# Half of a cross-attention's probabilities transposed by VectorE and five DMAs through DRAM, in place of TensorE

## The chip, the cores and the metric

The kernel runs on one core of one Trainium2 chip, in one launch. The metric is the device time of that launch in microseconds (us). All arithmetic is in 32-bit floats.

A core has five engines, each with its own in-order stream of instructions: TensorE (PE in the profile; its weight loads are a second row, PEld), VectorE (DVE), ScalarE (ACT), GpSimd (POOL) and SyncE (SP, which here only issues DMAs). They wait for each other through semaphores. SBUF is the on-chip memory of 128 partitions, PSUM the accumulators that TensorE writes, in banks of 512 floats a partition.

## The reference

Sixteen sequences, each with 128 queries of width 512 and a context of 2048 rows of width 512. Three layers follow each other:

```
x = x + xattn(layernorm(x), ctx)      # 16 heads of 32; k, v from ctx
x = x + mamba_and_mlp(layernorm(x))   # selective scan of 16 states, then an MLP of 2048
x = x + moe(layernorm(x))             # one shared and one gated expert product
# inside xattn, per sequence and head:
attn = softmax(q @ k.T * scale)       # 128 x 2048
out  = attn @ v                       # 128 x 32
```

What the change touches is `attn @ v`. It sums over the 2048 context rows, so the exponentials, which come out of the softmax with queries on partitions, must be turned until context rows lie on partitions.

## The kernel before

**Steps.** One loop, `for u in range(last)`, writes the whole order of work by hand; no scheduler moves an instruction afterwards. The first 256 steps (NU) are the attention: step u takes sequence u // 16, context block u // 4 % 4 of 512 rows, and head group u % 4 of four heads (`split`). Beside it, step u carries pieces of everything else: the k and v projections of the next context block (a seven-product scheme in place of eight, line 240), the Mamba layer of earlier pairs of sequences (input projection, scan), and after step 256 the MLP and the experts. From step 54 on (32 + LAG), each step also holds a piece of a scan. Dictionaries (`late`, `inner`, `middle`, `loads` and others) say in which step each piece goes; many pieces return every 32 steps, and below r is u % 32.

**One step on TensorE**, in order: the scores of four heads, one bank each (line 302); the weighting of the step before (`weighted(u - 1)`, line 346); two products of a projection (`x_products`, line 240, into `pa` and `pc`); sixteen transposes of 128x128, four to a bank (`turn`, line 333, a matrix product with the identity); the step's `late` pieces (line 531: Mamba's input projection; line 472: the output projection; line 716: Mamba's output; line 459: factors turned; line 399: queries); then `y_products`, one product in odd steps and two in even ones (line 240 again).

**One step on the others.** VectorE: the maxima of the four heads (line 310), the first half of the scan (687, its product with C at 690, a small memset at 666), the sum that empties `pc` (`x_sums`: line 260 for k, 270 for v), one of the four turned chunks copied out of PSUM (336), the second half of the scan, then sums of the projection and odds and ends. ScalarE: four exponentials (320), a copy that empties `pa` (280), the decays of the scan (673), three turned chunks (338), and every fourth step a copy of the weighted sums `avp` (360). GpSimd: differences of context tiles (232), the scan's inputs (652) and the sums of its outputs (703).

**SP's queue** is in order too. A step's loads stand at the top of the step, among them `load_bc` (601, two rows of 512 KB), context tiles (154), and weights into six shared buffers `ws` (504, 509, 167, 169). A load into a buffer still in use makes SP wait for the engine that uses it, and everything behind it in SP's queue waits too.

**Banks.** Four banks `s0` to `s3` hold a step's scores, then its turned chunks; `late` pieces borrow them in between, and the accumulator bank `avp` is borrowed in one step of four.

Of the kernel before, what the change touches and what calls it, by code (L numbers as in the profile page):

```python
# [8 lines left out]
FP = mybir.dt.float32  # L9
# [6 lines left out]
P = 128  # L16
B, NQ, D, S = 16, 128, 512, 2048
H, HD = 16, 32
KC = D // P
# [6 lines left out]
GT = GB * NQ  # L26
# [2 lines left out]
MT = MB * NQ  # L29
NE = 7  # L30
NH = 4


@with_exitstack
def perceiver_layer(ctx: ExitStack, tc: tile.TileContext, a: dict, out: bass.AP):
    nc = tc.nc

    const = ctx.enter_context(tc.tile_pool(name="const", bufs=1))
    dram = ctx.enter_context(tc.tile_pool(name="dram", bufs=1, space=DRAM))

    ident = const.tile([P, P], FP, tag="ident", name="ident")
# [14 lines left out]
    zd = [dram.tile([NQ, D], FP, tag=f"zd{b}", name=f"zd{b}") for b in range(B)]  # L56
    xnd = [dram.tile([NQ, D], FP, tag=f"xnd{b}", name=f"xnd{b}") for b in range(B)]
    bcd = [dram.tile([2 * DS, GT], FP, tag=f"bcd{g}", name=f"bcd{g}") for g in range(B // GB)]

    mv = const.tile([P, B, 2], FP, tag="mv", name="mv")  # L60
    rstd = const.tile([P, B], FP, tag="rstd", name="rstd")
# [43 lines left out]
    NU = B * SB * 4  # L105
# [3 lines left out]
    with ExitStack() as es:  # L109
        acon = es.enter_context(tc.tile_pool(name="acon", bufs=1))  # L110
        keep = es.enter_context(tc.tile_pool(name="keep", bufs=2))
        ssm = es.enter_context(tc.tile_pool(name="ssm", bufs=2))
        psum = es.enter_context(tc.tile_pool(name="psum", bufs=1, space=PSUM))
        att = es.enter_context(ExitStack())
        pool = att.enter_context(tc.tile_pool(name="att", bufs=2))
# [19 lines left out]
        scale = float(HD) ** -0.5  # L135
        nc.vector.tensor_scalar_mul(bq, bq, scale)

        ctx_t, kts, vts, qts, prs, pts, avs, stats, xts = ({} for _ in range(9))
# [43 lines left out]
        def split(u):  # L182
            return u // 16, u // 4 % 4, u % 4
# [92 lines left out]
                product(of, g, i, ps)  # L276

        def hold(key, g, pa, tag):
            t = pool.tile([P, 2, 256], FP, tag=tag, name=f"{tag}{key}{g}", bufs=1)
            nc.scalar.copy(t, pa)  # L280
            held[key] = t

# [43 lines left out]
                )  # L326
            prs[u] = pr

        def turn(u, i, bank):

            ps = heads(banks[bank])
            for j in range(4):
                nc.tensor.transpose(ps[:, j, :], prs[u][:, j, i * P : (i + 1) * P], ident)  # L333
            pT = pool.tile([P, 4, P], FP, tag="pT", name="pT", bufs=4)
            if i == 2 and u % 16 > 2:
                nc.vector.tensor_copy(pT, ps)  # L336
            else:
                nc.scalar.copy(pT, ps)  # L338
            pts[u, i] = pT

        def weighted(u):

            b, sb, hg = split(u)
            for i in range(4):
                for j in range(4):
                    nc.tensor.matmul(  # L346
                        avp[j * HD : (j + 1) * HD, hg, :],
                        vts[u // 4, hg // 2, i // 2][
                            :, i % 2, hg % 2 * P + j * HD : hg % 2 * P + (j + 1) * HD
                        ],  # L350
                        pts[u, i][:, j, :],
                        start=(i == 0),
                        stop=(i == 3),
                    )
            for i in range(4):
                del pts[u, i]
            del prs[u]
            if hg == 3:
                t = keep.tile([P, 4, P], FP, tag="avs", name=f"avs{b}_{sb}", bufs=4)
                nc.scalar.copy(t, avp)  # L360
                avs[b, sb] = t


        def moments_of(b):
# [21 lines left out]
        def turned(b, ps):  # L386
            xn = xts.pop((b, "n"))
            for kc in range(KC):
                nc.tensor.transpose(heads(ps)[:, kc, :], xn[:, kc * P : (kc + 1) * P], ident)
            xnT = keep.tile([P, KC, P], FP, tag="fx", name="xnT", bufs=3)  # L390
            nc.vector.tensor_copy(xnT, heads(ps))
            xts[b, "t"] = xnT

# [55 lines left out]
        fxs = {}  # L449

        def spread_out(b, sb):
            fx = keep.tile([P, H, HD], FP, tag="fx", name="fx", bufs=3)
# [110 lines left out]
        def silu_first(g, ec, ts):  # L563

            v = ts[g, ec]
            t = ssm.tile([P, GT], FP, tag="sg", name="sg", bufs=4)
# [591 lines left out]
        early = {}  # L1158
        late, after, inner, middle, loads, head, behind, between = ({} for _ in range(8))

        def put(where, u, f):
            where.setdefault(u, []).append(f)

        for b in range(B):
            s = 16 * b
            if b:
                put(loads, s - 8, lambda b=b: load_x(b))
                put(loads, s - 5, lambda b=b: load_w(0, b))
                put(inner, s - 8, lambda b=b: moments_of(b))
                put(middle, s - 7, lambda b=b: root_of(b))  # L1170
                put(inner, s - 7, lambda b=b: normal(b))
                put(late, s - 4, lambda ps, b=b: queries(b, ps))
            e = s + 16
            put(loads, e + 5, lambda b=b: load_w(3, b))
            put(inner, e - 1, lambda b=b: joined(b))
            put(inner, e, lambda b=b: joined_first(b))
            put(middle, e + 1, lambda b=b: shares(b))
            put(inner, e + 1, lambda b=b: joined_second(b))
            put(head, e + 2, lambda b=b: joined_third(b))
            for sb in range(SB):  # L1180
                put(inner, e + 2 + (sb > 0), lambda b=b, sb=sb: spread_out(b, sb))
                put(late, e + 3 + (sb > 0), lambda ps, b=b, sb=sb: scaled(b, sb, ps))
            put(late, e + 6, lambda ps, b=b: attended(b, ps))
            put(middle, e + 7, lambda b=b: root_of(b))
            put(inner, e + 7, lambda b=b: normed(b))
            put(late, e + 8, lambda ps, b=b: z_turned(b, ps))
# [38 lines left out]
        put(inner, NU, lambda: give_back(flat(pa)))  # L1225


        ways = (("k", pa, pc, "u2"), ("v", halves(banks[0]), halves(banks[1]), "u2v"))

        def first_products(of, ph):  # L1230
            x_products(of, 0, ph, *dict((w[0], w[1:3]) for w in ways)[of])
# [33 lines left out]
            y_sums(of, 0, 0, sa, sc, tag)  # L1265
        load_w(3, -1)

        bvx = keep.tile([P, KC, P], FP, tag="fx", name="bvx", bufs=3)
# [16 lines left out]
        for u in range(last):  # L1285
# [33 lines left out]
            for f in early.get(u, ()):  # L1319
                f()  # L1320
            if u == NU + 8:
                load_wex()
            for f in head.get(u, ()):
# [27 lines left out]


            after_turns = late.get(u, ())
            places = [banks[(3 + i) % 4] for i in range(len(after_turns))]
            if live and after_turns:
# [9 lines left out]
            taken = sum(any(p is b for b in banks) for p in places)  # L1365
# [105 lines left out]
```

## Time and profile before

| | |
|---|---|
| runs | 3762.42, 3763.41, 3765.85 us (median 3763.41) |
| profiled execution, first to last instruction | 3760.5 us; no time of its own around that is recorded, and the median is 2.9 us above it |
| scores of step 0, scores of step 255 (start) | 41.1 us, 3075.3 us |
| mean step, u from 96 to 127 | 12.19 us |
| busy time of VectorE in such a step | 9.75 us |
| granted TensorE clock | 0.998 of full speed |
| DMA | 548.42 MB, 146 GB/s over the span |

The profile has rows by group (line, engine, operation, output and inputs; count; busy time and mean ns of one; idle time before and what ended it), a timeline in order of time, windows (busy time of each engine in a stretch) and rows by DMA issue (count, KB, median us from issue to landing). A mean of one instruction includes its overlap with the next: four maxima of 683 ns each take 2.48 us together. Where two groups share an engine, the timeline's start times give the true pace.

### The profile page before, as it was taken

How to read it: one execution, taken by the hardware profiler on the slowest of the kernel's cores; microseconds unless marked ns; L12 is line 12 of the kernel's file. 1: busy time of each engine (PE TensorE's matmuls, PEld its weight loads, DVE VectorE, ACT ScalarE, POOL GpSimd, SP SyncE). 2: the span in 40 equal slices, each digit the busy share in tenths (PEclk: the TensorE clock that was granted, in tenths of full speed). 3: DMA queues.
4: the chain of work that ended last, by engine and by line, in shares of the span. 5: the costliest groups of instructions: out<-in, count | busy, mean ns of one | idle time of the engine just before them, and what ended most of it. 6: DMA issues, size and time to landing. Idle time of an engine off the chain costs nothing.

```text
span 3760.5 us, 70389 instructions
## 1 busy us (share of the span) xinstructions
PE 3722.9 (99%) x26120; PEld 2851.7 (76%) x26120; DVE 2706.2 (72%) x4854; ACT 2446.9 (65%) x5848; POOL 2112.4 (56%) x1969
## 2 busy tenths in 40 slices
PE   9999999999999999999999999999999999999999
PEld 7878787778777887888787878787778776655655
DVE  3444445887878777877788778877887877778843
ACT  4555556777767776777677767776777775545431
POOL 2111213676767666765666666766675667567820
PEclk9999999999999999999999999999999999999999
DMA  3111122344444535353534453445444448676752
GB/s 102 35 40 43 49 71 83 127 152 150 132 165 142 158 115 186 124 165 116 190 124 149 136 184 128 150 135 172 141 151 139 162 166 312 205 267 244 248 191 82
DMA packets 343225, 548.42 MB, mean 146 GB/s; under 512 B 24368, under 2 KB 227408, under 8 KB 342624
## 3 DMA queue, kind: packets, MB, share of 16 engines
q1 hardware_dynamic: 342432, 543.27, 43.5%
q8 instruction: 206, 3.38, 0.4%
q14 instruction: 139, 1.14, 0.1%
q0 software_dynamic: 448, 0.63, 0.1%
HBM read 527.29 MB, written 16.52 MB: 145 GB/s over the span
## 4 chain that ended last, share of the span: by engine, by line
PE 94%; DVE 2%; DMA 1%; ACT 1%; issue 1%; POOL 0%; SPq 0%; DVEq 0%; ACTq 0%; POOLq 0%
PE pa L240 24%; PE pc L240 17%; PE bank L333 12%; PE bank L302 7%; PE avp L346 7%; PE bank L531 5%; PE bank L942 4%; PE bank L911 2%; PE bank L1043 2%; PE bank L472 2%; PE avp L399 1%; PE bank L716 1%; PE pc L716 1%; PE avp L942 1%; PE pa L911 1%; PE pc L531 1%
## 5 line engine op out<-in xcount | busy, mean ns | idle before, releaser
L310 DVE TENSOR_REDUCE nm<-bank 128x1 f32<-128x512 f32 x1024 | 635.5, 683 | 225.2 <-PE bank L302 225.0
L703 POOL TENSOR_TENSOR ysum<-ysum,w 128x512 f32<-128x512 f32 x384 | 500.2, 1303 | 487.4 <-DVE hst L666 309.0
L320 ACT ACTIVATE pr<-bank,nm 128x512 f32<-128x512 f32 x1024 | 690.6, 688 | 90.9 <-DVE nm L310 85.3
L652 POOL TENSOR_TENSOR w<-dx,bc 128x512 f32<-128x512 f32 x512 | 655.9, 1302 | 8.9
L687 DVE TENSOR_TENSOR_SCAN hst<-hst,w 128x512 f32<-128x512 f32 x459 | 561.1, 1222 | 42.8 <-ACT hst L673 33.6
L338 ACT COPY pT<-bank 128x512 f32<-128x512 f32 x816 | 434.4, 586 | 177.2 <-PE bank L333 173.2
L673 ACT ACTIVATE hst<-dt,alog 128x254 f32<-128x254 f32 x918 | 439.4, 479 | 112.0 <-DVE hst L666 95.8
L333 PE MATMUL bank<-ident,pr 128*128 128x128 f32 x4096 | 508.2, 273 | 3.3 <-ACT pr L320 2.8
L333 PEld LDWEIGHTS bank<-ident,pr 128*128 128x128 f32 x4096 | 468.2, 141 | 47.1 <-issue 11.1
L346 PEld LDWEIGHTS avp<-pT,v 128*32 128x32 f32 x8192 | 208.0, 109 | 194.4 <-issue 176.6
L690 DVE TENSOR_TENSOR w<-hst,bc 128x512 f32<-128x512 f32 x459 | 317.4, 692 | 20.8 <-DMA bc<-bcd 5.2
L232 POOL TENSOR_TENSOR t<-c,c 128x512 f32<-128x512 f32 x128 | 163.1, 1274 | 257.6 <-PE pc L240 253.5
L302 PE MATMUL bank<-kt,qT 32*128 32x512 f32 x2048 | 296.0, 641 | 0.5 <-ACT pT L338 0.5
L346 PE MATMUL avp<-pT,v 128*32 128x128 f32 x8192 | 276.7, 276 | 0.0
L240 PE MATMUL pa<-t,ks 128*128 128x256 f32 x1024 | 248.6, 386 | 0.0
L240 PE MATMUL pa<-vs,t 128*128 128x256 f32 x1008 | 244.7, 386 | 0.0
L240 PEld LDWEIGHTS pa<-vs,t 128*128 128x128 f32 x1008 | 185.4, 190 | 34.6 <-issue 10.1
L240 PEld LDWEIGHTS pa<-t,ks 128*128 128x128 f32 x1024 | 184.8, 190 | 35.2 <-issue 11.6
L320 ACT ACTIVATION_READ_ACCUMULATOR pr<-bank,nm 128x1 f32 x1024 | 210.2, 205 | 0.0
L336 DVE COPY pT<-bank 128x512 f32<-128x512 f32 x208 | 143.9, 692 | 87.3 <-PE bank L333 85.6
L531 PE MATMUL bank<-zT,win 128*128 128x256 f32 x808 | 185.1, 379 | 0.0
L232 POOL TENSOR_TENSOR t<-c,t 128x512 f32<-128x512 f32 x128 | 163.7, 1279 | 36.1 <-issue 19.2
(320 smaller groups left out, 6889.0 us busy)
## 6 DMA issues: line engine op xcount, KB each, us to landing
bc<-bcd SPq DMA_DIRECT2D x512, 512.0 KB, 4.3
c<-in_ctxT_dram SPq DMA_DIRECT2D x256, 256.0 KB, 4.4
wf<-in_w_dram SPq DMA_DIRECT2D x124, 512.0 KB, 6.8
wqo<-in_wqkvo_dram SPq DMA_DIRECT2D x128, 256.0 KB, 4.8
win<-in_win_dram SPq DMA_DIRECT2D x128, 256.0 KB, 4.3
wout<-in_wout_dram SPq DMA_DIRECT2D x128, 256.0 KB, 4.2
x<-in_x_dram SPq DMA_DIRECT2D x16, 256.0 KB, 4.0
x1d<-x SPq DMA_DIRECT2D x16, 256.0 KB, 2.1
```

The lines of the kernel that those rows point to most:

```text
L240: nc.tensor.matmul(ps[:, r, :], l[:, kc, r * P : (r + 1) * P], m[:, kc, :], start=(i in (1, 2, 5) and r == 0 and kc == 0), stop=(r == 1 an ...
L302: nc.tensor.matmul(banks[j], qts[b][rows, hg, :], kts[u // 4, hg][rows, :], start=True, stop=True)
L310: nc.vector.tensor_reduce(stats[b][0][j][:, sb, hg : hg + 1], banks[j], AX.X, ALU.max, negate=True)
L320: nc.scalar.activation(pr[:, j, :], banks[j], AF.Exp, bias=nm[j][:, sb, hg : hg + 1], accum_out=sm[:, sb, h : h + 1],)
L333: nc.tensor.transpose(ps[:, j, :], prs[u][:, j, i * P : (i + 1) * P], ident)
L338: nc.scalar.copy(pT, ps)
L346: nc.tensor.matmul(avp[j * HD : (j + 1) * HD, hg, :], vts[u // 4, hg // 2, i // 2][:, i % 2, hg % 2 * P + j * HD : hg % 2 * P + (j + 1) * HD],
L531: nc.tensor.matmul(ps, w[:, kc, :], zTs[g][:, kc, :], start=(kc == 0), stop=(kc == KC - 1))
L652: nc.gpsimd.tensor_tensor(w, dx.unsqueeze(1).to_broadcast([P, NH // 2, GT]), bcs[g * 32 + r, 0][:, i * NH // 2 : (i + 1) * NH // 2, :], AL ...
L673: nc.scalar.activation(bt(h[:, k, :])[:, :, 1:], bt(dt)[:, :, 1:], AF.Exp, scale=aneg[:, ec, n : n + 1],)
L687: nc.vector.tensor_tensor_scan(flat, flat, w.rearrange("p n t -> p (n t)"), 0.0, ALU.mult, ALU.add)
L703: nc.gpsimd.tensor_tensor(s, s, w, ALU.add)
```

## The change

Of each step's four heads, heads 0 and 1 (NP = 2) are still turned by TensorE. Heads 2 and 3 (ND = 2) take another way:

- `blocks(u)`: two VectorE instructions, one for each head, transpose the 128x512 exponentials in blocks of 32x32 into a tile `tr`, and one DMA writes `tr` (512 KB) to one of two DRAM tiles. It stands after the first half of the scan and before `x_sums` in VectorE's order.
- `gathered(u)`: one step later, right behind `weighted(u)`, four DMAs read it back (128 KB each, onto 32 partitions, in rows of 1 KB) so that the 32x32 blocks lie as a full transposition would have put them, in `pd`.
- `weighted(u, js)`: heads 2 and 3 are weighted one step later than heads 0 and 1. `pd` has one buffer, so a step's gathers wait for the weighting that stands just ahead of them.

What follows from the lag: the values of heads 2 and 3 of each fourth step are kept by two GpSimd copies (`values_kept`); `avp` is copied out by three ScalarE instructions, the last a step later. `turn` now fills a bank with one head's four chunks, and all copies out are ScalarE's: two a step in place of three on ScalarE and one on VectorE. `late` pieces use banks 2 and 3, which the turns leave free. Three buffers shrink (`fx` from 3 to 2, `sg` from 4 to 2), and one of the four factor transpositions (`scaled`) moves from the steps with u % 16 = 4 to those with u % 16 = 5.

```diff
+    trd = [dram.tile([P, ND * 512], FP, tag=f"trd{i}", name=f"trd{i}") for i in range(2)]
...
-        def turn(u, i, bank):
-
-            ps = heads(banks[bank])
-            for j in range(4):
-                nc.tensor.transpose(ps[:, j, :], prs[u][:, j, i * P : (i + 1) * P], ident)
-            pT = pool.tile([P, 4, P], FP, tag="pT", name="pT", bufs=4)
-            if i == 2 and u % 16 > 2:
-                nc.vector.tensor_copy(pT, ps)
-            else:
-                nc.scalar.copy(pT, ps)
-            pts[u, i] = pT
+        def blocks(u):
+            t = pool.tile([P, 4, ND, 4, 32], FP, tag="tr", name=f"tr{u}", bufs=1)
+            for h in range(ND):
+                nc.vector.transpose(
+                    t[:, :, h].rearrange("p c i q -> p i c q"),
+                    prs[u][:, NP + h, :].rearrange("p (i c k) -> p i c k", i=4, c=4),
+                )
+            nc.sync.dma_start(trd[u % 2], t.rearrange("p c h i q -> p (c h i q)"))
+
+        def gathered(u):
+            pd = pool.tile([P, 4, ND, 4, 32], FP, tag="pd", name=f"pd{u}", bufs=1)
+            for c in range(4):
+                nc.sync.dma_start(
+                    pd[c * 32 : (c + 1) * 32].rearrange("k a h i q -> k a (h i q)"),
+                    trd[u % 2].rearrange("(a k) (c r) -> c k a r", k=32, c=4)[c],
+                )
+            pds[u] = pd
+
+        def turn(u, j):
+            ps = heads(banks[j])
             for i in range(4):
-                for j in range(4):
+                nc.tensor.transpose(ps[:, i, :], prs[u][:, j, i * P : (i + 1) * P], ident)
+            pT = pool.tile([P, 4, P], FP, tag="pT", name="pT", bufs=NP)
+            nc.scalar.copy(pT, ps)
+            pts[u, j] = pT
...
+        def weighted(u, js):
+            for i in range(4):
+                for j in js:
+                    v = u if j < NP else u - 1
+                    if v < 0 or v >= NU:
+                        continue
                     nc.tensor.matmul(
-                        avp[j * HD : (j + 1) * HD, hg, :],
...
-                        pts[u, i][:, j, :],
+                        avp[j * HD : (j + 1) * HD, v % 4, :],
+                        values(v, i, j),
+                        pts[v, j][:, i, :] if j < NP else pds[v][:, :, j - NP, i, :],
                         start=(i == 0),
                         stop=(i == 3),
                     )
...
-                nc.scalar.copy(t, avp)
+                nc.scalar.copy(t[:, 0:3, :], avp[:, 0:3, :])
+                nc.scalar.copy(t[0 : NP * HD, 3, :], avp[0 : NP * HD, 3, :])
...
-                put(inner, e + 2 + (sb > 0), lambda b=b, sb=sb: spread_out(b, sb))
-                put(late, e + 3 + (sb > 0), lambda ps, b=b, sb=sb: scaled(b, sb, ps))
+                put(inner, e + 2 + (sb + 1) // 2, lambda b=b, sb=sb: spread_out(b, sb))
+                put(late, e + 3 + (sb + 1) // 2, lambda ps, b=b, sb=sb: scaled(b, sb, ps))
...
             if 1 <= u <= NU:
-                weighted(u - 1)
+                weighted(u - 1, range(4))
+                if u > 1:
+                    weighted_last(u - 2)
+                weighted_out(u - 1)
+                gathered(u - 1)
+            for f in early.get(u, ()):
+                f()
             if u == NU:
+                weighted(NU, range(NP, 4))
+                weighted_last(u - 1)
...
             if scans:
                 scan(g, r, 0)
+            if live:
+                blocks(u)
+            if live and u % 4 == 2:
+                values_kept(u // 4)
             if makes:
                 hold(of, made, pa, "u1")
...
             if live:
-                for i in range(3 if taken else 4):
-                    turn(u, i, i)
+                for j in range(NP):
+                    turn(u, j)
...
-            if live and taken:
-                turn(u, 3, (3 + taken) % 4)
```

More of the change, by code (lines that the diff above doesn't have):

```diff
@@ L31 @@
 NH = 4
+ND = 2
+NP = 4 - ND
 @with_exitstack
@@ L136, in perceiver_layer @@
         nc.vector.tensor_scalar_mul(bq, bq, scale)
-        ctx_t, kts, vts, qts, prs, pts, avs, stats, xts = ({} for _ in range(9))
+        ctx_t, kts, vts, qts, prs, pts, avs, stats, xts, pds, vhs = ({} for _ in range(11))
         wfac, cfac, held = {}, {}, {}
@@ L278, in hold @@
         def hold(key, g, pa, tag):
-            t = pool.tile([P, 2, 256], FP, tag=tag, name=f"{tag}{key}{g}", bufs=1)
+            n = ND if tag == "tr" else 1
+            t = pool.tile([P, 2 * n, 256], FP, tag=tag, name=f"{tag}{key}{g}", bufs=1)[:, 0:2, :]
             nc.scalar.copy(t, pa)
@@ L327, in exps @@
             prs[u] = pr
-        def turn(u, i, bank):
-            ps = heads(banks[bank])
-            for j in range(4):
-                nc.tensor.transpose(ps[:, j, :], prs[u][:, j, i * P : (i + 1) * P], ident)
-            pT = pool.tile([P, 4, P], FP, tag="pT", name="pT", bufs=4)
-            if i == 2 and u % 16 > 2:
-                nc.vector.tensor_copy(pT, ps)
-            else:
-                nc.scalar.copy(pT, ps)
-            pts[u, i] = pT
-        def weighted(u):
-            b, sb, hg = split(u)
-            for i in range(4):
-                for j in range(4):
-                    nc.tensor.matmul(
-                        avp[j * HD : (j + 1) * HD, hg, :],
-                        vts[u // 4, hg // 2, i // 2][
-                            :, i % 2, hg % 2 * P + j * HD : hg % 2 * P + (j + 1) * HD
-                        ],
-                        pts[u, i][:, j, :],
+        def blocks(u):
[6 more added lines that the diff above has]
+            nc.sync.dma_start(trd[u % 2], t.rearrange("p c h i q -> p (c h i q)"))
@@ new lines, in values_kept, with values @@
+        def values_kept(n):
+            t = pool.tile([P, 4, ND * HD], FP, tag="vh", name=f"vh{n}", bufs=1)
+            for c in range(2):
+                nc.gpsimd.tensor_copy(
+                    t[:, 2 * c : 2 * c + 2, :], vts[n, 1, c][:, :, P + NP * HD : 2 * P]
+                )
+            vhs[n] = t
+        def values(u, i, j):
+            n, hg = divmod(u, 4)
+            if hg == 3 and j >= NP:
+                return vhs[n][:, i, (j - NP) * HD : (j - NP + 1) * HD]
+            at = hg % 2 * P + j * HD
+            return vts[n, hg // 2, i // 2][:, i % 2, at : at + HD]
@@ L354, in weighted, with weighted_out, weighted_last @@
                     )
-            for i in range(4):
-                del pts[u, i]
-            del prs[u]
+        def weighted_out(u):
+            b, sb, hg = split(u)
             if hg == 3:
                 t = keep.tile([P, 4, P], FP, tag="avs", name=f"avs{b}_{sb}", bufs=4)
-                nc.scalar.copy(t, avp)
+                nc.scalar.copy(t[:, 0:3, :], avp[:, 0:3, :])
+                nc.scalar.copy(t[0 : NP * HD, 3, :], avp[0 : NP * HD, 3, :])
                 avs[b, sb] = t
+        def weighted_last(u):
+            b, sb, hg = split(u)
+            if hg == 3:
+                nc.scalar.copy(avs[b, sb][NP * HD :, 3, :], avp[NP * HD :, 3, :])
         def moments_of(b):
@@ L389, in turned @@
                 nc.tensor.transpose(heads(ps)[:, kc, :], xn[:, kc * P : (kc + 1) * P], ident)
-            xnT = keep.tile([P, KC, P], FP, tag="fx", name="xnT", bufs=3)
+            xnT = keep.tile([P, KC, P], FP, tag="fx", name="xnT", bufs=2)
             nc.vector.tensor_copy(xnT, heads(ps))
@@ L451, in spread_out @@
         def spread_out(b, sb):
-            fx = keep.tile([P, H, HD], FP, tag="fx", name="fx", bufs=3)
+            fx = keep.tile([P, H, HD], FP, tag="fx", name="fx", bufs=2)
             nc.gpsimd.tensor_copy(fx, stats[b][:, sb, :].unsqueeze(2).to_broadcast([P, H, HD]))
@@ L565, in silu_first @@
             v = ts[g, ec]
-            t = ssm.tile([P, GT], FP, tag="sg", name="sg", bufs=4)
+            t = ssm.tile([P, GT], FP, tag="sg", name="sg", bufs=2)
             nc.scalar.activation(t, v, AF.Abs)
@@ L1225, in perceiver_layer @@
         put(inner, NU, lambda: give_back(flat(pa)))
-        ways = (("k", pa, pc, "u2"), ("v", halves(banks[0]), halves(banks[1]), "u2v"))
+        ways = (("k", pa, pc, "u2"), ("v", halves(banks[0]), halves(banks[1]), "tr"))
         def first_products(of, ph):
@@ L1266, in perceiver_layer @@
         load_w(3, -1)
-        bvx = keep.tile([P, KC, P], FP, tag="fx", name="bvx", bufs=3)
+        bvx = keep.tile([P, KC, P], FP, tag="fx", name="bvx", bufs=2)
         nc.vector.tensor_copy(bvx, bv.unsqueeze(2).to_broadcast([P, KC, P]))
@@ L1318, in perceiver_layer @@
                 open_ffn()
-            for f in early.get(u, ()):
-                f()
             if u == NU + 8:
@@ L1353, in perceiver_layer @@
             after_turns = late.get(u, ())
-            places = [banks[(3 + i) % 4] for i in range(len(after_turns))]
-            if live and after_turns:
+            free = banks[NP:]
+            places = [(free + banks)[i] for i in range(len(after_turns))]
+            if live and len(after_turns) > len(free):
                 if u % 4 == 0:
@@ L1364, in perceiver_layer @@
                 after_turns, places = (), ()
-            taken = sum(any(p is b for b in banks) for p in places)
             if live:
-                for i in range(3 if taken else 4):
-                    turn(u, i, i)
+                for j in range(NP):
+                    turn(u, j)
             if scans:
```

## The prediction

> **What bounds the kernel now.** I read the page's first part, then windows cut at the start of each step's scores, then the chain of waits, then the timeline.
>
> ```profile
> span 3760.5 us, 70389 instructions
> PE 3722.9 (99%) x26120; PEld 2851.7 (76%) x26120; DVE 2706.2 (72%) x4854; ACT 2446.9 (65%) x5848; POOL 2112.4 (56%) x1969
> ...
> L333 PE MATMUL bank<-ident,pr 128*128 128x128 f32 x4096 | 508.2, 273 | 3.3 <-ACT pr L320 2.8
> ```
>
> TensorE is busy 99% of the span, and its transposes waited 3.3 us in all. A busy PE may hide waits, so the windows of four steps (r = 0, 1, 29, 30; columns: length, then busy us and counts of PE, PEld, DVE, ACT, POOL):
>
> ```profile
> 1141.03:1151.97 10.94, 10.94 (x90) 8.82 (x89) 10.17 (x21) 8.43 (x20) 6.71 (x6) 1.00 0.43 154
> 1151.97:1161.18 9.21, 9.21 (x82) 7.30 (x81) 8.35 (x15) 7.79 (x19) 8.90 (x10) 1.00 0.26 92
> ...
> 1501.38:1510.59 9.21, 9.21 (x81) 7.30 (x81) 7.27 (x12) 7.14 (x17) 7.71 (x8) 1.00 0.46 162
> 1510.59:1521.53 10.94, 10.94 (x90) 8.83 (x89) 9.20 (x17) 7.63 (x18) 7.00 (x7) 1.00 0.32 103
> ```
>
> Steps with the same TensorE work take the same time whatever VectorE does beside them (9.21 with 7.27 us of VectorE and with 8.35): TensorE's own work sets the step. The chain of waits agrees, and gives each part's pace:
>
> ```profile
> 1505.46 1.73 PE pc L240 x8
> 1507.18 1.75 PE bank L333 x16
> 1508.93 1.73 PE pa L240 x8
> 1510.66 1.07 PE bank L302 x8
> 1511.73 1.01 PE avp L346 x32
> ```
>
> Sixteen transposes take 1.75 us, 0.109 each. But VectorE is busy 9.75 us of a mean step of 12.19 in the scan's part, so what it gains in work must be laid beside that.
>
> **What goes.** Eight transposes a step: 8 x 0.109 = 0.875 us, over 256 steps **224 us**. ScalarE and VectorE lose two copies a step of 0.59 and 0.69 us; ScalarE was off the path.
>
> **What comes on VectorE.** Two 128x512 transpositions; the trace has none. From below: half a pass, as 128x256 takes 0.45 us (line 633). From above: 1.22 (the scan, the slowest 128x512 in number) or 1.32 (line 808). Nearest are the passes of 128x512 at 0.68 to 0.69 (lines 310, 336, 690), which run 2.48 us for four. I take **0.65** each, 1.30 a step. The copy of 0.62 that goes stood behind `x_sums`; the new work stands ahead of it. That matters in even steps:
>
> ```profile
> 1511.75 2.48 DVE L310 TENSOR_REDUCE nm<-bank 128x1 f32<-128x512 f32 x4 [0.52 <-PE bank L302]
> ...
> 1514.15 1.22 DVE L687 TENSOR_TENSOR_SCAN hst<-hst,w 128x512 f32<-128x512 f32 x1
> ...
> 1515.40 0.69 DVE L690 TENSOR_TENSOR w<-hst,bc 128x512 f32<-128x512 f32 x1
> ...
> 1516.50 0.88 DVE L260 SCALAR_TENSOR_TENSOR kt<-pc,bk,u1k 128x256 f32<-128x256 f32 x2 [0.27 <-PE bank L333]
> ...
> 1517.97 1.89 PE L240 MATMUL pc<-c,ks 128*128 128x256 f32 x8
> ```
>
> Counted from the scores at 1510.59: maxima start at 1.16, the half scan is through at 5.64, the sum that empties `pc` ends at 6.79, and TensorE wants `pc` at 7.38. New: TensorE wants it at 7.38 - 0.875 = 6.5; VectorE has it ready at 5.64 + 1.30 + 0.88 = 7.8. TensorE waits 1.3 us and the step takes 7.8 + 3.56 (from that product to the next scores) = 11.4 against 10.94: **the even steps with nothing late in them get longer**. I did this sum for each of the 32 steps, carrying VectorE's lag over: the maxima start at 1.16 or when VectorE is free, new work is the window's VectorE time + 1.30 - 0.62 (no copy to remove at u % 16 of 0 to 2). Waits come out at r = 30 (1.7 us), 0 (1.1), 2 (2.8: step 1 holds 8.35 + 1.30 of VectorE in 8.33), 8, 24 and 26 (0.7 each), 7.7 us a cycle; the other steps have late pieces or only one product. 202 steps are 6.3 cycles: **49 us given back**. Before step 54 there is no scan and next to nothing waits: 3 us, at u % 4 = 0, where exponentials follow the copy of `avp`. The turned factors moved from u % 16 = 4, where VectorE now sets the time, to 5, where TensorE does: 4 x 0.109 in 14 pairs, **5 us**.
>
> [...] No row here shows the instruction.
>
> Does GpSimd hold it up? Some VectorE instructions do stand longer beside a GpSimd one:
>
> ```profile
> 751.29 1.28 POOL L703 TENSOR_TENSOR ysum<-ysum,w 128x512 f32<-128x512 f32 x1 [2.99 <-DVE hst L666]
> 751.59 1.46 DVE L422 COPY nm<-nm 128x16 f32<-128x16 f32 x4
> ```
>
> Copies of 16 columns, median 0.175, the first here 1.0, until GpSimd's sum ends; line 376 (128x512, SBUF to SBUF) has a mean of 0.94 where 0.69 is the rule. A transposition held likewise takes 0.94, and the same sum gives back 47 us more.
>
> **What comes on the queues.** A write of 512 KB and four reads of 128 KB, 256 times: 268 MB beside 548. DMA's 43.5% would grow by about half; it is no bound on average.
>
> ```profile
> bc<-bcd SPq DMA_DIRECT2D x512, 512.0 KB, 4.3
> c<-in_ctxT_dram SPq DMA_DIRECT2D x256, 256.0 KB, 4.4
> ...
> x<-x1d SPq DMA_DIRECT2D x16, 256.0 KB, 7.1
> ```
>
> A gather is issued after the weighting ends, 2.2 us into a step; four issues of 0.4 put the last start at 3.6, and at 4.3 to land it is there at 7.9. TensorE needs it at 8.33 + 1.2 = 9.5 in the shortest step, an odd one. Cover: 1.6 us, so **nothing**, but a landing of over 5.9 uses it up.
>
> In two steps of 32 the cover is gone, because SP stands at loads ahead of the gathers until TensorE's late pieces free the `ws` buffers (r = 11, scores at 1266.70; r = 22, scores at 1407.43):
>
> ```profile
> 1275.57 2.27 SPq L504 DMA_DIRECT2D win<-in_win_dram  x2
> ...
> 1412.14 6.84 SPq L509 DMA_DIRECT2D wout<-in_wout_dram  x6
> ```
>
> r = 11: SP is through with `win` at 11.1, now about 10.6 as late pieces start 0.5 earlier; a `bc` load, then gathers at 11.3 to 12.5, landed at 16.8; step 11 now ends at 12.2 and the weighting wants them at 13.4: a wait of 3.4. r = 22: `wout` is through at 11.6, then `dtw`, `bc`, gathers to 13.5, landed at 18; wanted at 14.7: 3.3. There are seven of the first (g = 0 to 6) and six of the second: **44 us**. At r = 12 the step is 17 us long and hides it. After the last step the gather of head group 255 is waited for outright: about **4 us**.
>
> Half of the weighting's moving operands now lie in four pieces of 32. The trace has no such row; between nothing and half of 1.01 us more a step (129 us); I take nothing, as the same elements stream.
>
> **Sum:** 224 - 49 - 3 - 5 - 44 - 4 = 119 us. From the profiled 3760.5 that is 3641.5, and with the 2.9 us that the median lies above it **3644**.
>
> **Rivals.**
> 1. *The gathers land late in ordinary odd steps too.* Each writes 32 partitions, a quarter of what any load here does. For: the reads of scratch tensors at 7.1 (x1d), the write just ahead, half as much traffic again. Against: `bc` and `c`, 4.3 and 4.4. At twice 4.3, TensorE waits 2.7 us in five odd steps of 32, 2.3 in three, 1.8 in two: 24 a cycle, eight cycles, 191 us, of which some 30 replace waits of the even steps: **3805**, slower. It decides against the change from a landing of about 8 us on.
> 2. *The transposition is slower than a pass*: at 0.94, **3691**; at 1.22 the even steps give back 172 in place of 49: 3767, no change.
> 3. *VectorE's waits are shorter and the gathers land soon*: at 0.45 a transposition, 18 us less, and without the 44: **3582**.
>
> **How the numbers follow.** Forecast 0.52 (3600 to 3690), rival 1 0.20, rival 2 0.18, rival 3 0.10. Of rival 2, 0.10 is faster, 0.04 within 0.2% and 0.04 slower; of rival 1, 0.01 ends within 0.2%. Hence 0.72 faster by over 0.2%, 0.05 within (about what a measurement of this kernel can tell from no change), 0.23 slower. The range 3590 to 3800 leaves out some 0.07 below and 0.13 above.
>
> **What would show it.** The two VectorE instructions at 0.6 to 0.7 us. Odd steps of 8.3 us. In even steps without late pieces, about 11.4 us, with the first `y_products` waiting for line 260's or 270's successor. Waits of TensorE on `pd` at r = 12 and r = 23 of 3 to 4 us and nowhere else. Wrong would be: a landing of the gathers of over 6 us, waits on `pd` in most odd steps, or 9.21-us steps that do not shrink at all.

## The result and the profile after

The changed kernel takes **3814.81 us** (median, 3811.22 to 3817.92) where the kernel before, run beside it, takes 3762.91: a ratio of **1.0139, 95% interval 1.0124 to 1.0153**. It is 1.4% slower; forecast were 3644 us. The profiled execution has a span of 3816.1 us.

First the totals of the page, and the group of the new instruction (busy time, mean ns of one, idle before):

```profile
span 3816.1 us, 69166 instructions
...
PE 3602.9 (94%) x24072; PEld 2678.4 (70%) x24072; DVE 2862.3 (75%) x5158; ACT 2304.2 (60%) x5672; POOL 2139.1 (56%) x2097
...
L338 DVE STREAM_TRANSPOSE tr<-pr 128x512 f32<-128x512 f32 x512 | 338.8, 696 | 85.3 <-ACT pr L325 75.9
```

The 2048 transposes are gone from TensorE (26120 matmuls to 24072), yet its busy time fell by 120 us only, not by 224, and it is now idle in 6% of the span. A VectorE transposition has a mean of 0.696 us. Next the four steps that the prediction showed (r = 0, 1, 29, 30; the columns are those of its windows), and r = 6:

```profile
1122.38:1133.67 11.29, 10.32 (x81) 7.98 (x80) 11.07 (x21) 7.38 (x19) 6.68 (x7) 1.00 0.70 213
1133.67:1142.01 8.34, 8.34 (x74) 6.43 (x73) 7.50 (x13) 7.04 (x18) 8.03 (x8) 1.00 0.80 257
1497.16:1505.50 8.34, 8.34 (x74) 6.43 (x73) 7.07 (x12) 6.88 (x17) 8.11 (x8) 1.00 0.51 171
1505.50:1516.97 11.47, 10.32 (x81) 7.97 (x80) 10.34 (x19) 7.05 (x17) 8.13 (x11) 1.00 0.92 293
1186.26:1206.12 19.86, 16.57 (x89) 10.37 (x88) 12.71 (x25) 8.41 (x20) 17.18 (x18) 0.91 0.54 176
```

The odd steps are 8.34 us and the even ones 11.29 and 11.47, as forecast (8.3 and 11.4). But r = 6 holds eight matmuls fewer than before and takes 19.86 us where it took 14.37, and the column after POOL's says that TensorE had 0.91 of its clock in it. TensorE's waits (us in total, times, longest) say who ended them:

```profile
PE avp L386 <- DMA pd<-trd: 65.1, 21, 4.8
PE bank L516 <- POOL aT L511: 34.0, 13, 2.8
PE pc L244 <- DVE kt L264: 30.5, 25, 2.5
PE pc L663 <- DVE v L274: 22.9, 32, 0.9
PE pc L244 <- DVE v L274: 12.9, 24, 1.0
PE bank L307 <- DVE avs L510: 5.4, 12, 0.5
```

The first line is the forecast wait for the gathers, longer than forecast. The second and the last belong to the moved turned factors: the output projection (line 516) waits for GpSimd's sum, and the scores for the bank that VectorE empties late. The fourth is the first product of the step widths (`dt_first`). These three were not in the forecast; the third and the fifth are the even steps' waits, which were.

By stage: steps 2 to 53 take 545.9 us for 580.5 (forecast: some 541); steps 54 to 254 take 2517.0 for 2436.2. Mean step lengths there, over five cycles of 32 ("forecast" is before minus 0.88 plus the wait that the prediction gives it):

| r | before | forecast | after | over the forecast |
|---|---|---|---|---|
| 6, 22 | 14.37, 14.37 | 13.49, 13.49 | 18.78, 18.49 | 5.3, 5.0 |
| 12, 23 | 17.96, 16.51 | 20.5, 18.9 | 23.93, 22.48 | 3.4, 3.5 |
| 25 | 16.08 | 15.2 | 17.86 | 2.7 |
| 3, 7, 19, 27, 31 | 10.08, 9.64, 10.08, 9.64, 9.64 | 0.88 less | 9.91 each | 4.9 together |
| 2 | 11.08 | 13.0 | 14.15 | 1.2 |

Together some 26 us a cycle, 6.3 cycles: 164 of the 171 us by which the forecast missed.

The median landing is as short as forecast (SP's issues, KB each, median us from issue to landing), though 262 of the 1024 gathers took more than 6 us, up to 8.4:

```profile
trd<-tr SPq DMA_DIRECT2D x256, 512.0 KB, 3.0
pd<-trd SPq DMA_DIRECT2D x1024, 128.0 KB, 3.9
```

### The profile page after: what moved, and what is told of

Same layout as the page of the kernel before. It is cut to its first block, busy times and chain, and to the rows that moved or that the text cites. A ratio compares the mean times of both kernels' runs of the same rounds, so it can differ in the third digit from the quotient of the medians.

```text
span 3816.1 us, 69166 instructions
## 1 busy us (share of the span) xinstructions
PE 3602.9 (94%) x24072; PEld 2678.4 (70%) x24072; DVE 2862.3 (75%) x5158; ACT 2304.2 (60%) x5672; POOL 2139.1 (56%) x2097
## 5 line engine op out<-in xcount | busy, mean ns | idle before, releaser
L338 DVE STREAM_TRANSPOSE tr<-pr 128x512 f32<-128x512 f32 x512 | 338.8, 696 | 85.3 <-ACT pr L325 75.9
L734 DVE TENSOR_TENSOR w<-hst,bc 128x512 f32<-128x512 f32 x459 | 317.2, 691 | 19.3 <-DMA bc<-bcd 3.5
L307 PE MATMUL bank<-kt,qT 32*128 32x512 f32 x2048 | 308.6, 641 | 8.1 <-DVE avs L510 5.4
L360 ACT COPY pT<-bank 128x512 f32<-128x512 f32 x512 | 272.0, 582 | 56.1 <-PE bank L358 56.1
L386 PE MATMUL avp<-pT,v 128*32 128x128 f32 x4096 | 288.4, 282 | 1.2 <-ACT pT L360 1.1
L386 PE MATMUL avp<-pd,v 128*32 128x128 f32 x3072 | 215.9, 285 | 57.0 <-DMA pd<-trd 57.0
L358 PE MATMUL bank<-ident,pr 128*128 128x128 f32 x2048 | 265.7, 273 | 0.8 <-ACT pr L325 0.7
L358 PEld LDWEIGHTS bank<-ident,pr 128*128 128x128 f32 x2048 | 238.8, 141 | 25.3 <-ACT pr L325 1.8
L244 PE MATMUL pa<-vs,t 128*128 128x256 f32 x1008 | 254.5, 397 | 0.0
L575 PE MATMUL bank<-zT,win 128*128 128x256 f32 x992 | 224.8, 379 | 0.0
L262 ACT ACTIVATE kt<-pa,bk 128x256 f32<-128x256 f32 x128 | 53.6, 470 | 263.7 <-PE pa L244 263.7
```

Source lines behind the costliest of these rows:

```text
L244: nc.tensor.matmul(ps[:, r, :], l[:, kc, r * P : (r + 1) * P], m[:, kc, :], start=(i in (1, 2, 5) and r == 0 and kc == 0), stop=(r == 1 an ...
L307: nc.tensor.matmul(banks[j], qts[b][rows, hg, :], kts[u // 4, hg][rows, :], start=True, stop=True)
L338: nc.vector.transpose(t[:, :, h].rearrange("p c i q -> p i c q"), prs[u][:, NP + h, :].rearrange("p (i c k) -> p i c k", i=4, c=4),)
L358: nc.tensor.transpose(ps[:, i, :], prs[u][:, j, i * P : (i + 1) * P], ident)
L386: nc.tensor.matmul(avp[j * HD : (j + 1) * HD, v % 4, :], values(v, i, j), pts[v, j][:, i, :] if j < NP else pds[v][:, :, j - NP, i, :], st ...
L734: nc.vector.tensor_tensor(w, h, bcs[g * 32 + r, DS][:, i * NH // 2 : (i + 1) * NH // 2, :], ALU.mult)
```

## The experiments

The theory before them: three separate losses (the factors' place; the gathers' place behind loads; the transpositions' place ahead of the sum), each made larger by half a clock on TensorE after a wait (its granted clock reads 0.50, in the changed kernel for 3.4 us and more). Ratios are to the kernel before, run beside each.

### The factors back in their steps

```diff
-                put(inner, e + 2 + (sb + 1) // 2, lambda b=b, sb=sb: spread_out(b, sb))
-                put(late, e + 3 + (sb + 1) // 2, lambda ps, b=b, sb=sb: scaled(b, sb, ps))
+                put(inner, e + 2 + sb // 2, lambda b=b, sb=sb: spread_out(b, sb))
+                put(late, e + 3 + sb // 2, lambda ps, b=b, sb=sb: scaled(b, sb, ps))
```

That is two and two of the four factors, with the two buffers of the change; the kernel before, with three, has one and three.

> Only the turned factors are moved back to the two steps they had before (two blocks at u % 16 = 3, two at u % 16 = 4; the buffers of two stay). Theory (the changed kernel is slower because the fourth factor, a step later, meets the output projection: TensorE waits 2.8 us for GpSimd's sum, and the scores wait for the bank): the steps at r = 6 and r = 22 fall from 18.8 and 18.5 to 13.5 to 14, r = 5 and 21 from 8.8 to 8.3, and the whole to 3740 to 3765. Rival (those steps are long for the late lag of VectorE alone, whatever the factors do): r = 6 and 22 stay above 17 us and the whole is at 3795 to 3815.

Measured: 3777.93 us, ratio 1.0040 (1.0025 to 1.0055); 37 us came back, less than expected. The waits for GpSimd's sum and for the bank are gone, r = 5 and 21 are at 8.34, but r = 6 and 22 only fell to 15.6. A wait of 1.7 us for `pd` has taken their place. In SP's queue of this kernel (step r = 5 begins at 1167.07) the gathers stand behind four loads of `wqo`, and the DMA engines' share was 1.07 right then (last columns: clock, DMA share, GB/s):

```profile
1163.29 2.52 SPq L158 DMA_DIRECT2D c<-in_ctxT_dram  x3
1165.86 1.92 SPq L173 DMA_DIRECT2D wqo<-in_wqkvo_dram  x4
1167.96 0.51 SPq L645 DMA_DIRECT2D bc<-bcd  x1
1169.29 2.67 SPq L348 DMA_DIRECT2D pd<-trd  x4
```

```profile
1169.30:1172.00 2.70, 2.70 (x13) 2.39 (x14) 2.67 (x5) 2.67 (x8) 2.62 (x3) 1.00 1.07 401
```

The four gathers landed 7.3 to 8.2 us after their issue, the last at 1178.3, where the median of this kernel is 3.7; TensorE went on at 1178.4. So the theory holds for the cause, and a second wait stood behind the first.

### The gathers ahead of the loads

```diff
-            for f in loads.get(u, ()):
-                f()
+            if u > NU or u < 1:
+                for f in loads.get(u, ()):
+                    f()
...
                 gathered(u - 1)
+                for f in loads.get(u, ()):
+                    f()
```

(Step 0 and the steps after the last head group keep the old place.)

> Only the order in SP's queue is changed: in each step up to the last the four gathers stand ahead of that step's weight loads. Theory (the gathers wait behind loads that wait for buffers, and each wait of 4 us is paid for a second time by the half clock that follows it): the waits on pd at r = 12, 23 and 25 go; those steps fall from 23.9, 22.5 and 17.9 to about 17.1, 16.5 to 17.0 and 15.2, and the whole is at 3705 to 3730. Rival 1 (no clock in it: only the wait itself is got back, 4.1 us at r = 12 and at r = 23 and 1.0 at r = 25): 3755 to 3765. Rival 2 (the gathers land late for the traffic of the loads beside them, not for their place): waits on pd at r = 12 and 23 stay over 2 us and the whole is at 3790 or more.

Measured: 3741.33 us, ratio 0.9942 (0.9927 to 0.9957): **73 us** came back, between the theory's 85 to 110 and the first rival's 50 to 60. r = 12 falls to 17.09, exactly the step without a wait: 6.84 us came back there for a wait of 4.28. The wait on `pd` falls from 65.1 us to 6.2. r = 23 falls to 17.14, 1.5 us above the step without a wait, and r = 25 does not fall (18.14 for 17.86): both now wait for `wout` (15.9 us in all). At r = 23 its last two loads are issued from 7.6 us into the step (8.0 in the kernel before), but land 3.7 to 6.4 us after their issue, where they took 2.6 to 3.2. So the second rival, traffic, is refuted for the gathers at r = 12 and 23, and what it names shows in the loads that were put behind them. This edit alone makes the changed kernel faster than before.

### The transpositions behind the sum

```diff
-            if live:
-                blocks(u)
...
                 x_sums(of, made, phase, pa, pc)
+            if live:
+                blocks(u)
```

> Only VectorE's order is changed: the two transpositions stand behind the sum that empties pc rather than ahead of it. Theory (that sum comes 1.3 us later and TensorE's next products, and the first product of the step widths at u % 4 = 3, wait for it): waits for the sums fall from about 66 us in all to under 15, even steps without late pieces are at 10.1 to 10.3 instead of 11.3, r = 3, 7, 19, 27, 31 lose 0.7 to 1.1, and the whole is at 3735 to 3755. Rival (VectorE is the bound of those steps, and what is moved behind the sum delays the next maxima by as much): even steps stay at 11 us or more, and the whole is within 15 us of 3815.

Measured: 3798.79 us, ratio 1.0093 (1.0076 to 1.0109); only 16 us came back. The steps that the theory named did get shorter (r = 24, 26, 30 to 10.5, 10.5 and 10.6; r = 7, 27, 31 to 9.0), about 8 us a cycle, but r = 10, 23, 25 and 28 got longer, r = 25 from 17.86 to 20.07. Neither side was right: VectorE did not bound the steps that got shorter, but the write to scratch memory came later with the transpositions, and in SP's queue the loads that the projection issues stand behind it (at u = 121, r = 25, the write went from 7.5 to 12.1 us into the step and the loads from 9.0 to 12.5). The waits on `pd` rose to 85.4 us; at r = 25 they are 0.8 us longer and the clock withholds 1.0 more. How the later queue leads to them was not followed.

### All three

> The factors moved back, the gathers ahead of the loads, the transpositions behind the sum: all three in one kernel. Theory (the three are separate losses and add up): 3570 to 3610, faster than before by 4 to 5%. Rival (the three hide one another: VectorE's lag takes over in the even steps and the waits on pd return as the steps get shorter): 3680 to 3760.

Measured: 3697.17 us, ratio 0.9819 (0.9794 to 0.9845), faster than before by 1.8%. The gains add up (37 + 73 + 16 = 126, measured 118), but short of 3570 to 3610. What is left is in the waits of this kernel, and in SP's queue in step r = 23, which begins at 1361.63:

```profile
PE bank L760 <- DMA wout<-in_wout_dram: 37.0, 12, 4.3
PE pc L244 <- DVE kt L264: 15.9, 20, 2.7
PE avp L386 <- DMA pd<-trd: 13.4, 10, 4.9
```

```profile
1363.51 0.33 SPq L342 DMA_DIRECT2D trd<-tr  x1
...
1369.12 1.75 SPq L348 DMA_DIRECT2D pd<-trd  x4
1370.92 0.43 SPq L183 DMA_DIRECT2D xn<-xnd  x1
1371.45 0.39 SPq L342 DMA_DIRECT2D trd<-tr  x1
1371.93 2.81 SPq L553 DMA_DIRECT2D wout<-in_wout_dram  x2
```

The projection's last two loads of `wout` were issued from 8.0 us into the step before the change, here from 10.3. Ahead of them stand the gathers, and these read what the step before wrote: its write, itself behind six loads of `wout`, was issued at 1363.51 and landed 5.5 us later, just ahead of 1369.12. In all six steps r = 23 of this kernel from step 64 on the gathers start 0.05 to 0.07 us after such a landing. The write of the step itself adds 0.5 us in front of the loads; its transpositions had been done for 1.1 us. And the loads then take 4.4 to 6.4 us to land, where they took 2.6 to 3.2.

### The factors' move alone, on the kernel before

```diff
-                put(inner, e + 2 + (sb > 0), lambda b=b, sb=sb: spread_out(b, sb))
-                put(late, e + 3 + (sb > 0), lambda ps, b=b, sb=sb: scaled(b, sb, ps))
+                put(inner, e + 2 + (sb + 1) // 2, lambda b=b, sb=sb: spread_out(b, sb))
+                put(late, e + 3 + (sb + 1) // 2, lambda ps, b=b, sb=sb: scaled(b, sb, ps))
```

> The kernel before with one edit of the change: the fourth factor's spreading and scaling one step later (its four buffers of three stay three). Theory A (the move costs only because VectorE is late in the changed kernel, so that GpSimd's sum is not through when the output projection wants it): the wait for that sum at r = 6 and r = 22 is under 1 us and the whole is within 10 us of before. Theory B (the move costs by itself, the sum standing behind GpSimd's other work whatever VectorE does): the wait is 2 us or more in those steps, these steps grow by 3 us or more, and the whole is 20 to 50 us above before.

Measured: 3820.90 us, ratio **1.0153** (1.0138 to 1.0169): 58 us slower than before, as slow as the whole change. Theory B, and above its range. No VectorE transposition is in this kernel, so its lag is not the cause. GpSimd's queue shows it; first the kernel before (step r = 6 begins at 1203.82), then this one (1214.04), each with the sum into `aT` and what stands around it:

```profile
1193.63 4.11 POOL L467 TENSOR_TENSOR aT<-aT,avs 128x512 f32<-128x512 f32 x3
...
1208.30 2.63 POOL L703 TENSOR_TENSOR ysum<-ysum,w 128x512 f32<-128x512 f32 x2
```

```profile
1214.53 2.51 POOL L652 TENSOR_TENSOR w<-dx,bc 128x512 f32<-128x512 f32 x2
...
1217.68 2.62 POOL L703 TENSOR_TENSOR ysum<-ysum,w 128x512 f32<-128x512 f32 x2
...
1221.99 0.72 POOL L708 TENSOR_TENSOR zs<-ysum,zs 128x256 f32<-128x256 f32 x1
1222.67 1.26 POOL L467 TENSOR_TENSOR aT<-aT,avs 128x512 f32<-128x512 f32 x1
```

Before, three sums in a row are through by 1197.7, 6 us ahead of the step in which the projection reads `aT`. With the last factor a step later, its sum stands behind eight operations of the scan's part in this step and ends 9.9 us into step r = 6; TensorE is ready for it at 7.1. And the wait is not all (TensorE's timeline, then the window of the projection):

```profile
1219.67 1.47 PE L333 MATMUL bank<-ident,pr 128*128 128x128 f32 x12
1223.99 5.40 PE L472 MATMUL bank<-wqo,aT 128*128 128x512 f32 x8 [2.84 <-POOL aT L467]
```

```profile
1223.99:1229.39 5.40, 5.40 (x10) 2.33 (x11) 0.00 (x0) 0.00 (x0) 5.32 (x5) 0.68 0.00 0
```

Eight matmuls that took 3.60 us in the kernel before take 5.40 at a mean clock of 0.68. Of the 13 waits for this sum, 35.4 us in all, twelve are of 2.82 to 2.85 us and each of these is followed by half a clock: 35.4 and 12 times 1.8 make 57 us, where 58 were measured. In the changed kernel only four of the twelve such waits at r = 6 and 22 are (the last section has the counts), so some 20 of the 58 us belong to where the waits happen to fall.

### TensorE kept at work through the waits

```diff
+                for _ in range(7 if u >= 64 and u % 32 in (12, 23) else 0):
+                    weighted(u - 1, range(NP))
                 weighted(u - 1, range(4))
```

> The changed kernel with more work: in the steps u % 32 = 12 and 23 from u = 64 on, the matmuls of the two heads weighted at once are run seven times over before the real ones (7 x 16 matmuls, some 3.8 us by the 1.08 us that 32 take, inside waits of 4.1 to 4.4 us for pd); the repeats write the same sums again. Theory (a wait of about 4 us is followed by half clock, which makes such a step 1.8 to 2.5 us longer than the wait): with TensorE kept at work these steps fall by that, from 23.9 to 21.4 to 22.1 and from 22.5 to 20.3 to 20.9, and the whole by 20 to 28 us, to 3787 to 3795, though more is computed. Rival (no clock in it; the steps are long for the landing alone): both steps keep their length within 0.5 us or grow, and the whole is 3810 to 3825.

Measured: 3805.90 us, ratio 1.0114 (1.0094 to 1.0133): 9 us less than the changed kernel although it computes more, but less than half of what was expected. The first 16 products behind the weighting at r = 12 (u = 108), first in the changed kernel and then in this one:

```profile
1272.70:1276.94 4.24, 4.24 (x20) 3.65 (x19) 1.38 (x2) 4.13 (x13) 0.45 (x1) 0.87 0.01 2
```

```profile
1265.48:1269.20 3.72, 3.72 (x20) 3.26 (x19) 0.90 (x2) 3.57 (x12) 0.00 (x0) 1.00 0.00 0
```

The clock is whole and the products take 3.72 us, as in the kernel before. But the repeats overran the wait: by the timeline 110 matmuls of two heads take 6.2 us, where the 112 were reckoned at 3.8 from the rate of four heads, and r = 12 and 23 fell by only 0.7 us each. A shorter block was therefore tried, five repeats:

> The changed kernel with the repeats of the two heads' weighting in the steps u % 32 = 12 and 23, five in place of seven: with seven, 16 matmuls took 0.87 us and the block ended 0.7 us after the changed kernel's weighting, though no half clock followed and the 16 products behind it took 3.7 us in place of 4.2 to 4.7. Five are some 4.4 us, about the wait of 4.1 to 4.4. Theory (the half clock after the wait costs 1.4 to 2.3 us a step): those steps fall to 21.2 to 22.4 at r = 12 and 20.0 to 21.0 at r = 23, and the whole to 3785 to 3800. Rival (no gain from a TensorE kept at work): the steps keep their length within 0.4 us and the whole is within 8 us of 3815.

Measured: 3797.01 us, ratio 1.0084 (1.0070 to 1.0097): **18 us faster than the changed kernel, with more work in it**; r = 12 at 22.3 us and r = 23 at 20.6, both as expected. (The profiled run took 3814.56 us, the other five 3792 to 3798: in it r = 6 and 22 are longer than in the changed kernel, 20.0 and 19.0.) From the first product that reads `pd` to the end of the step, r = 12 takes 16.0 us here, exactly as in the kernel with the gathers ahead of the loads, and 18.2 in the changed kernel. Half a clock after a wait is thus a cost of its own, here 2.2 us in this step, and not a sign of something else.

### The write behind the late pieces

```diff
-            nc.sync.dma_start(trd[u % 2], t.rearrange("p c h i q -> p (c h i q)"))
+            trs[u] = t.rearrange("p c h i q -> p (c h i q)")
...
+            if live:
+                nc.sync.dma_start(trd[u % 2], trs.pop(u))
             for f in behind.get(u, ()):
```

> The kernel of the three edits (factors back, gathers ahead of loads, transpositions behind the sum), and the write to scratch memory issued behind the step's late pieces rather than right after the transpositions. Theory (in SP's queue the write waits for VectorE's late transpositions, and the loads of wout that the projection at r = 23 and 25 issues stand behind it: 37 us of waits for wout in the kernel of three): those waits fall under 12 us, r = 23 falls from 21.6 to 16 to 17 and r = 25 from 19.0 to 15.3 to 16.3, and the whole from 3697 to 3640 to 3660. Rival (the projection waits for its loads because they land late for the gathers' traffic): r = 23 and 25 stay above 18.5 and the whole is within 12 us of 3697.

Measured: 3669.27 us, ratio 0.9753 (0.9737 to 0.9769): 28 us less than with all three, half of what was expected. The waits for `wout` fall from 37.0 to 22.5 us; r = 23 falls to 19.3 only and r = 25 stays at 19.0. The theory had taken the nearest link for the first: the gathers still wait for the landing of the write of the step before, and at u = 119 they start at 8.3 us and the loads at 10.6 and 11.1 (7.5, 10.3 and 12.8 with all three). The rival has a part in it too: at r = 23 these loads land 3.8 to 6.4 us after their issue. With the transpositions at their place in the change, ahead of the sum:

> As the last one (factors back, gathers ahead of loads, write behind the late pieces), but with the transpositions ahead of the sum, where the change has them. Theory (with the write out of the way of the loads, the place behind the sum is worth what it took out of the even steps and of u % 4 = 3, some 8 us a cycle of 32): 35 to 55 us slower than the last one. Rival (VectorE's time decides and only passes the wait on): within 15 us of the last one.

Measured: 3671.96 us, ratio 0.9758 (0.9743 to 0.9772): the same. The rival is right. Ahead of the sum, the waits for the sums are 62 us in all and those for `wout` 13; behind it, 25 and 22.5, and 11.6 for `pd` where there were 4.9. What one side gains the other loses.

### Both places, step by step

Ahead of the sum, but behind it in the six steps where that was shorter, all in one kernel:

```diff
+            behind_sum = u % 32 in (7, 24, 26, 27, 30, 31)
+            if live and not behind_sum:
+                blocks(u)
...
                 x_sums(of, made, phase, pa, pc)
+            if live and behind_sum:
+                blocks(u)
```

> Factors back, gathers ahead of loads, write behind the late pieces, and the transpositions ahead of the sum, but in six steps of 32 (u % 32 = 7, 24, 26, 27, 30, 31) behind it: those where the kernel with all of them behind was shorter. Theory (what is late in VectorE stays within a step and the next one, so the shorter lengths of both kernels can be had together): the six steps fall from 9.9, 11.3, 11.7, 9.9, 11.5 and 9.9 to 9.0, 10.5, 10.5, 9.0, 10.6 and 9.1, 5.3 us a cycle, and the whole is at 3630 to 3650. Rival (the lag is handed on to the next cycle's steps and to the projection's loads): r = 0, 2, 23 and 25 grow by what the six lose, and the whole is at 3660 to 3680.

Measured: 3661.51 us, ratio 0.9731 (0.9714 to 0.9747), 10 us less, a third of what was expected. The six steps fell as the theory said (r = 31 to 9.0, r = 7 to 9.0), and r = 0 and r = 8, the steps after two of them, rose from 11.3 to 13.5 and from 11.2 to 12.3, and r = 25 from 16.7 to 17.7: the rival's range, and its reason, that VectorE's lag is handed on. The softmax's small operations at the end of their step:

```diff
-            put(inner, e + 1, lambda b=b: joined_second(b))
-            put(head, e + 2, lambda b=b: joined_third(b))
+            put(inner, e + 2, lambda b=b: joined_second(b))
+            put(inner, e + 2, lambda b=b: joined_third(b))
```

> As the last one, with the four small VectorE operations on the softmax's sums moved from ahead of the maxima of the step u % 16 = 2 to its end. Theory (at r = 2 they stand ahead of the maxima and TensorE waits 2.5 us for the sum behind them): r = 2 falls from 13.8 to 11.5 to 12.7, and the whole by 6 to 15 us against the last one. Rival (GpSimd's spreading comes later by as much, and the scaling in the step after waits for it): r = 3 or r = 4 grow, and the whole is within 4 us of the last one or above it.

Measured: 3656.63 us, ratio 0.9717 (0.9702 to 0.9733). r = 2 fell from 13.5 to 11.5 and r = 3 and 4 stayed, so the place is right; of the 13 us that this makes in 6.3 cycles r = 25 took most back (17.7 to 19.7: 0.5 us more of waits for `wout`, and 1.7 of clock withheld behind them); the total shows 5 us, and the two intervals overlap. Last, without r = 7 and 31 in the list:

> As the last but one with the joined operations at the step's end, but the transpositions behind the sum in four steps of 32 only (24, 26, 27, 30), no longer at 7 and 31. Theory (what 7 and 31 gained, 0.9 us each, r = 8 and r = 0 gave back as 1.1 and 2.2, since the transpositions behind the sum delay the next step's maxima): r = 7 and 31 return to 9.9, r = 8 and 0 to 11.2 and 11.3, 1.5 us a cycle less, and the whole is 5 to 14 us under that kernel's 3657. Rival (r = 0 and r = 8 are late for the lag of the steps ahead, whichever step hands it on): r = 0 stays above 12.5 and the whole is within 4 us of 3657 or above.

Measured: **3641.58 us, ratio 0.9665 (0.9651 to 0.9679)**, 3.4% faster than before and the fastest of all. r = 0 and 8 are back at 11.3 and 11.2, at the price of 0.9 us at r = 31 and 0.7 at r = 7. What remains in its waits:

```profile
PE bank L762 <- DMA wout<-in_wout_dram: 21.0, 12, 3.1
PE pc L665 <- DVE v L274: 11.4, 14, 0.9
PE pc L244 <- DVE v L274: 11.1, 17, 1.4
PE pc L244 <- DVE kt L264: 9.4, 20, 1.2
```

The loads of `wout` at r = 23 and 25 are the largest; at r = 23 the gathers ahead of them still start right behind the landing of the last write (at u = 119 6.8 and 6.9 us into the step). Another queue for the gathers was not tried.

## Why the prediction was wrong, by its own steps

- **The step that failed first is "The turned factors moved from u % 16 = 4 ... to 5 ...: 4 x 0.109 in 14 pairs, 5 us".** It priced the four transposes (the product is 6.1, not 5) and not who reads what they lead to. Alone on the kernel before, the move costs 58 us; moved back in the changed kernel, 37 return. The prediction asked whether VectorE or TensorE sets the time of the two steps; what the move does on GpSimd, whose sum is the last link before line 516, it did not ask. The window of r = 6 in the kernel before shows GpSimd busy 13.82 of 14.37 us: a full queue, in which a later operation has no slack to fall into.
- **Waits were priced at their length.** The kernel before has next to no waits in its 256 steps, its mean clock is 0.998 and every window shown reads 1.00. Behind the steps its trace does have four waits of 2.0 to 3.7 us (ending at 3095.3, 3291.7, 3360.8 and 3664.4) that are each followed by 3.4 us at 0.50; the prediction gave them no price. In the changed kernel the mean is 0.980 of 3816 us: 76 us of clock withheld, 8 before (some of it while TensorE waited anyway). At r = 12 a wait of 4.28 us costs 6.84: the products that read `pd` start 4.7 us later, and all behind them takes 2.2 longer.
- **"3.4" and "3.3" behind blocked loads, 44 us:** right in place and mechanism, 4.3 and 4.4 in size; with the clock, 73 us (gathers ahead of the loads). r = 25, 2.7 us over the forecast, was not seen, and in every experiment on the changed kernel that step stayed over it (16.7 to 20.4 us).
- **The even steps, 49 us:** right in place and mechanism. Waits of 0.96, 2.5, 0.44, 0.5, 0.85 and 1.22 at r = 0, 2, 8, 24, 26, 30 make 6.5 us a cycle; forecast were 7.7. But the steps grew by more than their waits, by 0.2 to 0.3 us each and by 1.4 at r = 2 (half a clock): against before minus 0.88 they are 9.2 us a cycle longer. What was missed is that `dt_first` uses the same bank: it waits for the same sum at r = 3, 7, 19, 27, 31, 22.9 us in all.
- **224 us off TensorE, the pass of 0.65 us, no cost for the strided operand:** right. Odd steps are 8.34, two transpositions take 1.3 us, and 32 matmuls of the weighting still take 1.08.
- **Rival 1** (late landings in ordinary odd steps) is refuted: in those of 8.34 us the gathers land in 2.7 to 3.9 us (medians) and nothing waits for them. But landings of over 6 us, which the prediction called a sign of being wrong, are a quarter of all: at r = 5, 9, 13 and 21 the medians are 6.5 to 7.3 us. They cost next to nothing here, as these steps or those behind them are longer; with the factors moved back, such landings at r = 5 and 21 became the waits at r = 6 and 22. **Rival 2** is refuted by 0.696. **Rival 3** had a transposition of 0.45 us and no waits on `pd`; neither came. Of the 0.23 that the prediction gave to slower, nearly all was rival 1's, which was not the cause.
- **The gain itself was there.** With the order of the queues mended, the same division of the heads is 122 us faster than before, about the 119 that the sum gave. That the two agree is in part chance: the mended kernel has other waits than the sum had.

## What to carry to other kernels

When an edit frees a buffer by moving a piece a step later, follow its result to its last reader through every engine's queue: GpSimd, busy for 13.82 of the 14.37 us (96%) of step r = 6 before the change, gave the late sum no way forward, and with the move alone TensorE waited 2.84 us for it. A wait of TensorE can cost more than its length: at r = 12 one of 4.28 us cost 6.84. One DMA queue is one order: a new transfer that waits for an engine, or for another transfer to land, belongs behind the loads that do not. Where the gathers, waiting for a write to land, stood ahead of them, the last loads of `wout` were issued 10.3 us into r = 23 in place of 8.0, and the waits for `wout` came to 37.0 us.

## What the runs showed of the hardware

Half a clock after a wait was not expected. In the changed kernel's record of the granted clock it comes in stretches of 3.41, 6.83 or 13.65 us, each at 0.50 (the last one runs on past the end). From 400 us on, the starts of these stretches lie whole multiples of 3.413 us apart, to within 0.005. In the kernel before they do too: 3094.91, 3292.88, 3361.15 and 3664.93 us are 58, 20 and 89 times 3.413 apart.

Between 500 and 3000 us of the changed kernel such a stretch began during the wait, or within 2 us of its end, for none of 39 waits of TensorE of 0.7 to 1.5 us, for 2 of 4 of 1.5 to 2.0 us, for 8 of 17 of 2.0 to 3.0 us, and for all 11 longer ones. So the same wait may or may not be followed by it. Counted in pieces of 3.413 us, laid off from such a start (both traces, from 400 us on): 27 pieces at full clock held 2.0 us or more of idle TensorE (waits of over 0.15 us, added up), and all 27 were followed by half a clock; of 4 with 1.9 to 2.0 us 3 were, and of 1905 with less 2. Of the twelve waits for GpSimd's sum at r = 6 and 22 of the changed kernel (2.19 to 2.84 us), four have 2.05 to 2.59 us in one such piece, and these four were followed by half a clock; the other eight are cut in two, with 1.90 us at most in either piece, and at 793.85 us, for one, a wait of 2.84 us ends and the clock reads 1.00 behind it.

In the kernel with the factors' move alone, all twelve waits of 2.82 to 2.85 us were followed by half a clock, and the one of 1.3 us was not. These are counts of this case; they do not show what lowers the clock.
